# Attention stacks of 128 rows with zeros written by VectorE, and the last two second feed-forwards side by side

## The chip, the core and the metric

The kernel is one program on one core of a Trainium2 chip. A core has five engines, each with a queue of its own that runs in order: TensorE (PE; its weight loads are shown as PEld), VectorE (DVE), ScalarE (ACT), GpSimd (POOL) and SyncE (SP), which here only starts DMA transfers. Engines wait for each other through semaphores. The metric is the time of one execution on the device, in microseconds (us); lower is better. The profile is one execution, recorded instruction by instruction. For TensorE it also shows the granted clock, as a share of full speed: in this kernel it is 1.0 or 0.5.

## The reference

Four sequences of 512 tokens with 128 channels (`x`: 4 x 512 x 128, fp32) pass four blocks, each added to its input:

```python
def reference(x, ...):
    x = x + mamba_and_moe(layernorm(x))   # state-space scan, then 8 experts, top 2 of them per token
    x = x + ffn(layernorm(x))             # the first feed-forward
    x = x + attention(layernorm(x))       # 16 heads of 8 channels, causal
    x = x + ffn(layernorm(x))             # the second feed-forward, same weights
    return x

def ffn(x):                               # 128 -> 384 -> 128, weights are integers / 127
    h = silu(x @ wg.T) * (x @ wu.T)
    return h @ wd.T

def attention(x):                         # per head: scores against a latent of 64 channels
    c_kv = x @ W_dkv.T
    q_lat = einsum('bqhd,hdl->bhql', q, k_eff)
    attn = softmax(causal(einsum('bhql,bkl->bhqk', q_lat, c_kv) / sqrt(8)))
    return einsum('bhql,hld->bqhd', einsum('bhqk,bkl->bhql', attn, c_kv), v_eff)
```

## The kernel before

**Two stages.** The first stage (up to about 392 us) runs the scan: 64 steps, with the experts of finished groups of sequences ([0], then [1], then [2, 3]) and the first feed-forwards beside it. Its order on the engines is the program's. The second stage, lines 1078 to 1330, is attention; there a scheduler orders the instructions of each engine by what is ready and by priority, within what the program's order, tiles and buffers allow. Experts of the last group, the projections of the later sequences and the second feed-forwards run beside attention. They are generators in four lists (`closing`, `tokens`, `tiles`, `ends`), and each turn of a list runs its first generator up to its next `yield`.

**Attention** works in 8 units `u`, two per sequence, each with 8 heads of 512 positions. Before its units a sequence passes `project(b)`: layernorm (L153 to L167), a transposition (`transposed`, L172 to L182: into PSUM and back through ScalarE), products `pq` (L511) and `pu` (L521), and a split of the fp32 values into three bf16 parts (ScalarE L524, L525; GpSimd L526 to L528), which go out to HBM as `q_d` (L530) and `k_d` (L533).

- `fill(u)` (L1127) loads the parts back into two stacks, `qs[u % 3]` and `ks[u % 3]`: 9 parts x 8 channels = 72 rows (`NP9`). Six loads on SyncE's queue; each waits there until `q_d` or `k_d` is written, and what stands behind it waits too, expert weights among it.
- `maxima(u)`: score products `sc` over the 72 rows (L1145), a product that adds the causal mask (L1149), and the maximum of each row by VectorE (L1141). The maxima, split into three bf16 parts, are transposed, copied (`mT`, L1172), written to HBM (`m_d`, L1174) and loaded into three more rows of `qs`, 72 to 74 (L1175). The same rows of `ks` hold -1 (`below`, loaded once for each of the three stacks at the stage's start, L1103), so the product over 75 rows is the score less its maximum.
- `exps(G)`, two per unit with 4 heads each: `st` over 75 rows (L1198), the mask (L1206), the exponential by ScalarE (L1211); ten tiles each.
- `weigh(G)`: weighted sums `po` (L1225, 32 columns per head, fp32), a copy (L1235), transposition `pyt` (L1239), a copy (L1243), division (L1249, L1250), and after the last group of a sequence the sum `base` (L1255, GpSimd).

**The feed-forward** `ffn` (L428) is used twice per sequence. Per call: layernorm with an rsqrt of some ten small VectorE steps (L136 to L145, then `nm` L162) and four ScalarE steps `xn` (L167); `transposed` to `xT`; for each of three slices `pg` (L445), `pu` (L447), tanh (L449) and two VectorE steps (L321, L322); then 12 products `fpd` (L454), a copy (L459), a sum on GpSimd (L460). `last(b)` is the second feed-forward and ends with the store of the output (L468). A product in fp32 shows as two instructions in the profile.

**Order of the ends.** `begin = {3: (0,), 5: (1,), 7: (2,)}` adds `last(0)`, `last(1)` and `last(2)` to the list `ends` when units 3, 5 and 7 begin. `last(3)` runs alone at the end.

**Buffers.** The feed-forward takes its PSUM tiles from `ps_s` ("sc", two banks) and `ps` ("mm", one), its SBUF tiles from `wt`. `ps_q` ("sq") holds the score tiles of `maxima`, `ps_t` ("st") those of `exps`, two banks each.

At the stage's start VectorE also works on the end of the last sequence's scan part: `h` (L957), a norm with another rsqrt (L968, L136 to L145), the router's choice from its logits `lg` (L984, L1005 and after), and row numbers for the scatter to the experts (L252, L260).

Of the kernel before, what the change touches and what calls it, by code (L numbers as in the profile page):

```python
# [8 lines left out]
F32 = mybir.dt.float32  # L9
# [7 lines left out]
P = 128  # L17
# [20 lines left out]
def block_kernel(ctx, tc, x, rms1_w, rms2_w, in_proj_w, conv_w, conv_b, x_proj_w,  # L38
# [130 lines left out]
                scale=r[:, t : t + 1], bias=nm[:, t : t + 1],  # L169
            )  # L170

    def transposed(ps, dst, src, scale=None, beside=None):  # L172

        pt = ps.tile([P, L], F32, tag="mm" if ps is ps_m else "sc", name="pt")
        for t in range(NT):
            nc.tensor.transpose(pt[:, t * P : (t + 1) * P], src[:, t, :], ident)
            if beside:
                beside()
        if scale is None:
            nc.scalar.copy(dst, pt)  # L180
        else:
            nc.scalar.activation(dst, pt, AF.Copy, scale=scale)  # L182
# [17 lines left out]
    ]  # L200


    ps = ps_m = ctx.enter_context(tc.tile_pool(name="ps_m", bufs=1, space=PSUM))
    ps_s = ctx.enter_context(tc.tile_pool(name="ps_s", bufs=2, space=PSUM))
    wt = ctx.enter_context(tc.tile_pool(name="tiles", bufs=2))

# [218 lines left out]
        scaled(dst, src, r, less(mv[:, :, 0], r, NT))  # L425
        yield

    def ffn(src, dst):  # L428

        xn = wt.tile([P, NT, C], F32, tag="xn", name="xn", bufs=1)  # L430
        yield from layernorm(xn, src)
        xT = wt.tile([P, L], F32, tag="xT", name="xT", bufs=1)
        transposed(ps, xT, xn)
        yield
        hT = wt.tile([P, NHC, L], F32, tag="fh", name="fh", bufs=1)
        for f in range(NHC + 1):
            if f:
                halved(hT[:, f - 1, :], th, pg, pu)
            if f == NHC:
                yield  # L440
                break
            yield "sc"
            cols = slice(f * P, (f + 1) * P)
            pg = ps_s.tile([P, L], F32, tag="sc", name="pg")
            nc.tensor.matmul(pg, fwg[:, cols], xT, start=True, stop=True)  # L445
            pu = ps_s.tile([P, L], F32, tag="sc", name="pu")
            nc.tensor.matmul(pu, fwu[:, cols], xT, start=True, stop=True)  # L447
            th = wt.tile([P, L], F32, tag="th", name="th")
            nc.scalar.activation(th, pg, AF.Tanh, scale=0.5)  # L449
            yield  # L450
        pd = ps.tile([P, NT, C], F32, tag="mm", name="fpd")
        for t in range(NT):
            for f in range(NHC):
                nc.tensor.matmul(  # L454
                    pd[:, t, :], hT[:, f, t * P : (t + 1) * P], fwd[:, f, :],
                    start=(f == 0), stop=(f == NHC - 1),
                )
        o = wt.tile([P, NT, C], F32, tag="xn", name="fo", bufs=1)
        nc.scalar.copy(o, pd)  # L459
        nc.gpsimd.tensor_tensor(dst, src, o, ALU.add)  # L460
        yield
# [1 line left out]
    def first_ffn(b):  # L463
        yield from ffn(base[b], xs[b])

    def last(b):
        yield from ffn(base[b], base[b])
        nc.sync.dma_start(out[b].rearrange("(t p) c -> p t c", p=P), base[b])  # L468

    class Stream:  # L470
# [31 lines left out]
    def project(b):  # L502

        xn = wt.tile([P, NT, C], F32, tag="xn", name="axn", bufs=1)
        yield from layernorm(xn, xs[b])
        xT = wt.tile([P, L], F32, tag="xT", name="axT", bufs=1)
        transposed(ps, xT, xn)
        yield
        yield
        pq = ps.tile([P, L], F32, tag="mm", name="pq")  # L510
        nc.tensor.matmul(pq, w_qk[0], xT, start=True, stop=True)  # L511
        qk = wt.tile([P, L], F32, tag="qk", name="qk")
        nc.scalar.copy(qk, pq)
        yield
        q_d = dram0.tile([3, HS, NH, L], BF16, tag="q_d", name="q_d", bufs=2)
        k_d = dram0.tile([3, 3, HS, NH, L], BF16, tag="k_d", name="k_d", bufs=2)
        for half in range(2):
            yield
            rows = slice(half * KVL, (half + 1) * KVL)
            pq = ps.tile([P, L], F32, tag="mm", name="pu")  # L520
            nc.tensor.matmul(pq, w_up[rows, :], qk[rows, :], start=True, stop=True)  # L521
            full = wt.tile([P, L], F32, tag="full", name="full", bufs=1)
            parts = wt.tile([P, 3, L], BF16, tag="parts", name="parts", bufs=1)
            nc.scalar.copy(parts[:, 0, :], pq)  # L524
            nc.scalar.copy(full, pq)  # L525
            nc.gpsimd.tensor_tensor(full, full, parts[:, 0, :], ALU.subtract)  # L526
            nc.gpsimd.tensor_copy(parts[:, 1, :], full)
            nc.gpsimd.tensor_tensor(parts[:, 2, :], full, parts[:, 1, :], ALU.subtract)  # L528
            if half == 0:
                nc.gpsimd.dma_start(q_d.rearrange("j d h l -> (d h) j l"), parts)  # L530
            else:
                for j in range(3):
                    nc.gpsimd.dma_start(k_d[:, j].rearrange("i d h l -> (d h) i l"), parts)  # L533
            yield
        stores[b] = q_d, k_d, qk
# [63 lines left out]
    with ExitStack() as first:  # L599
# [110 lines left out]
        def front(b):  # L710
# [1 line left out]
            hn = wt.tile([P, NT, C], F32, tag="xn", name="hn", bufs=1)  # L712
            scaled(hn, xs[b], norms["r"][:, 1, b], norms["m"][:, 1, b])
            yield
            transposed(ps_s, hT[:, KW - 1 :], hn, r1w[:, 0, :], (lambda: warm(1)) if b == 0 else None)
            yield
            xi[b] = w2.tile([P, NE, L], F32, tag="xi", name=f"xi_{b}")
            sz[b] = w2.tile([P, NE, L], F32, tag="sz", name=f"sz_{b}")
# [217 lines left out]
        def close(b):  # L936
# [36 lines left out]
                )  # L973
            yield
            hsT = wt.tile([P, L], F32, tag="hsT", name="hsT", bufs=1)
            transposed(ps, hsT, hs[b], r2w[:, 0, :])
            yield
            pl = ps.tile([P, NT, NEXP], F32, tag="mm", name="pl")
            for t in range(NT):
# [46 lines left out]
        def warm(n):  # L1026

            pw = ps_x.tile([P, NE, L], F32, tag="bx", name="warm")
            for _ in range(n):
                nc.tensor.matmul(pw[:, 0, 0:P], ident, ident, start=True, stop=True)  # L1030
# [46 lines left out]
    with ExitStack() as second:  # L1077
# [15 lines left out]

        NP9 = 9 * HS
        NU = NH // 2
        UNITS = 2 * B
        qs, ks = [], []
        for i in range(3):  # L1100
            qs.append(w1.tile([96, NU, L], BF16, tag=f"qs{i}", name=f"qs{i}"))
            k = w1.tile([96, NU, L], BF16, tag=f"ks{i}", name=f"ks{i}")
            nc.sync.dma_start(  # L1103
                k[NP9 : NP9 + 3, :, :], below.unsqueeze(1).to_broadcast([3, NU, L])
            )
            ks.append(k)

        def values(b):
            va, qk = vs[b % 2], stores[b][2]
# [10 lines left out]
        def fill(u):  # L1120

            b, h0 = u // 2, (u % 2) * NU
            q_d, k_d, _ = stores[b]
            for i in range(3):
                at = slice(3 * HS * i, 3 * HS * (i + 1))
                for stack, of in ((qs[u % 3], q_d), (ks[u % 3], k_d[i])):
                    nc.sync.dma_start(  # L1127
                        stack[at], of[:, :, h0 : h0 + NU, :].rearrange("j d h l -> (j d) h l")
                    )

        def maxima(u):
# [4 lines left out]
            for t in range(NT):  # L1136
                w = (t + 1) * P
                n = L // w
                for h0 in range(0, NU, n):
                    if taken:  # L1140
                        nc.vector.tensor_reduce(*taken, AX.X, ALU.max)  # L1141
                    sc = ps_q.tile([P, L], F32, tag="sq", name="sc")
                    for h in range(h0, h0 + n):
                        c = (h - h0) * w
                        nc.tensor.matmul(  # L1145
                            sc[:, c : c + w], q[0:NP9, h, t * P : w], k[0:NP9, h, 0:w],
                            start=(h == h0), stop=False, skip_group_check=True,
                        )
                    nc.tensor.matmul(  # L1149
                        sc[:, 0 : n * w].rearrange("p (h k) -> p h k", k=w)[:, :, t * P : w],  # L1150
                        identb, maskq.unsqueeze(1).to_broadcast([P, n, P]),
                        start=False, stop=True, skip_group_check=True,
                    )
                    taken = (
                        mx[:, t, h0 : h0 + n], sc[:, 0 : n * w].rearrange("p (h k) -> p h k", k=w)
                    )
                    yield
# [14 lines left out]
            nc.scalar.copy(mT, pm)  # L1172
            m_d = dram.tile([3, NU, L], BF16, tag="m_d", name="m_d")
            nc.gpsimd.dma_start(m_d.rearrange("i h l -> (i h) l"), mT)  # L1174
            nc.gpsimd.dma_start(q[NP9 : NP9 + 3, :, :], m_d)  # L1175
            yield

        scale = float(HS) ** -0.5
# [2 lines left out]
        def exps(G):  # L1181
# [6 lines left out]
            for blocks in (  # L1188
# [7 lines left out]
                for j, kt, c in blocks:  # L1196
                    rows = slice(kt * P, (kt + 1) * P)
                    nc.tensor.matmul(  # L1198
                        pt[:, c : c + L - kt * P], k[0 : NP9 + 3, h0 + j, rows],
                        q[0 : NP9 + 3, h0 + j, kt * P : L],  # L1200
                        start=(c == 0), stop=False, skip_group_check=True,
                    )
                    got[j][kt] = p[:, c : c + L - kt * P]
# [77 lines left out]

        ends = Stream()
        streams = closing, tokens, tiles, ends
        begin = {3: (0,), 5: (1,), 7: (2,)}
        rate = {0: 0.7, 1: 0.7, 2: 0.7, 3: 0.7, 4: 0.7}
        filled, credit = 2, 0.0
        while 0 not in stores:
# [39 lines left out]
                run(more)  # L1327
        while any(stream.gens for stream in streams):
            turn(*streams)
        run(last(B - 1))  # L1330


# [54 lines left out]
```

## Time and profile before

| | us |
|---|---|
| median of 3 runs (lowest, highest) | 919.38 (919.25, 921.01) |
| the profiled execution | 916.44 |
| its span, first to last instruction | 914.7 |
| mean granted clock of TensorE | 0.872 |

The profile's page gives busy time and its share of the span per engine, and the span in 40 slices, where a digit is tenths. Two more rows of it, the busy slices of TensorE and of VectorE:

```
PE   8698697699898855976696998898768997799854
DVE  4799999899998987755364542275534266457311
```

A slice is 914.7 / 40 = 22.9 us. The scan fills slices 1 to 16, where VectorE is at 9 for long; attention is the rest. Other views are: groups of instructions (line, engine, operation, tile written and tiles read, partitions x elements, type, count, then busy time, mean ns of one, and idle time before with what ended it); the timeline of one engine (start, length, what, and in brackets the idle time before it and its releaser); stretches (length, busy time and count per engine in the order PE, PEld, DVE, ACT, POOL, then clock, DMA share, GB/s); and the chain of waits that ended last.

### The profile page before, as it was taken

What the parts mean: (1) busy time and instruction counts of PE and PEld (TensorE: products, weight loads), DVE (VectorE), ACT (ScalarE), POOL (GpSimd) and SP (SyncE); (2) the same over time, 40 slices, a digit from 0 to 9 for tenths busy, and PEclk for the clock granted to TensorE, in tenths of its full rate; (3) what the DMA queues carried; (4) which work ended last, traced back from release to release, by engine and by line L of the source; (5) the groups of instructions that cost most, each with busy time, mean ns of one, the idle gap of its engine ahead of it and who ended that gap; (6) DMA issues with size and microseconds to landing.
All of it is one profiled execution on the core that took longest, in us unless ns stands there. A gap on an engine that the chain in (4) does not pass through costs nothing. (4 is left out here: it accounts for less than half of the span.)

```text
span 914.7 us, 12164 instructions
## 1 busy us (share of the span) xinstructions
PE 736.9 (81%) x3867; PEld 436.0 (48%) x3867; DVE 584.6 (64%) x1160; ACT 409.4 (45%) x793; POOL 308.1 (34%) x242
## 2 busy tenths in 40 slices
PE   8698697699898855976696998898768997799854
PEld 4432242363466512564465576367524454365422
DVE  4799999899998987755364542275534266457311
ACT  3847556556743421342112553413436524546641
POOL 1165755765664467315103013000341402301010
PEclk9898999799999867998668999979968887989977
DMA  5167221361466314426735157627310420600000
GB/s 132 43 220 259 68 58 58 100 204 54 145 183 198 93 57 125 142 80 200 184 130 178 61 173 214 152 68 221 98 29 3 120 64 20 158 2 14 3 13 11
DMA packets 84481, 99.18 MB, mean 108 GB/s; under 512 B 10369, under 2 KB 56457, under 8 KB 83241
## 3 DMA queue, kind: packets, MB, share of 16 engines
q1 hardware_dynamic: 78881, 87.09, 32.4%
q0 software_dynamic: 4352, 10.89, 3.8%
q8 instruction: 31, 0.51, 0.2%
q10 hardware_dynamic: 1184, 0.43, 0.2%
q14 instruction: 33, 0.27, 0.1%
HBM read 76.67 MB, written 21.63 MB: 107 GB/s over the span
## 5 line engine op out<-in xcount | busy, mean ns | idle before, releaser
L922 POOL TENSOR_TENSOR hc<-hst,cs 128x1024 f32<-128x1024 f32 x64 | 150.7, 2355 | 132.1 <-issue 31.6
L867 PE MATMUL yp<-hc,ident 128*128 128x512 f32 x256 | 148.0, 708 | 48.6 <-POOL hc L922 47.4
L910 DVE TENSOR_TENSOR_SCAN hst<-da,bx 128x1024 f32<-128x1024 f32 x64 | 146.4, 2287 | 11.7 <-POOL hc L922 4.6
L1141 DVE TENSOR_REDUCE mx<-sc 128x1 f32<-128x384 f32 (+3 forms) x168 | 102.9, 636 | 59.5 <-PE sc L1149 57.4
L867 PEld LDWEIGHTS yp<-hc,ident 128*128 128x128 f32 x256 | 51.5, 216 | 129.4 <-POOL hc L922 89.3
L1211 ACT ACTIVATE p<-st 128x512 f32<-128x512 f32 x160 | 90.2, 598 | 30.0 <-PE st L1206 26.8
L847 ACT ACTIVATE da<-delta,A 128x512 f32<-128x512 f32 (+1 forms) x128 | 84.8, 714 | 34.3 <-DVE hst L910 26.6
L1145 PE MATMUL sc<-ks,qs 72*128 72x128 bf16 (+3 forms) x256 | 73.5, 347 | 14.8 <-DMA ks<-k_d 7.9
L321 DVE SCALAR_TENSOR_TENSOR thm<-thm,mpg 128x512 f32<-128x512 f32 x53 | 36.1, 681 | 68.1 <-ACT thm L382 68.0
L889 DVE TENSOR_TENSOR bx<-du,pb 128x1024 f32<-128x1024 f32 x64 | 78.2, 1223 | 2.0 <-PE pb L857 0.4
L376 PE MATMUL mpg<-xTm,wgu 128*128 128x128 f32 x424 | 66.9, 300 | 12.2 <-DMA wgu<-in_Wg_dram 7.7
L1198 PE MATMUL st<-qs,ks 75*128 75x512 bf16 (+3 forms) x256 | 63.6, 312 | 11.7 <-ACT p L1211 5.9
L376 PEld LDWEIGHTS mpg<-xTm,wgu 128*128 128x128 f32 x424 | 59.9, 212 | 21.9 <-issue 15.8
L1174 POOL DMA_DIRECT2D m_d<-mT x8 | 4.4, 552 | 183.6 <-ACT mT L1172 183.6
L376 PE MATMUL mpu<-xTm,wgu 128*128 128x128 f32 x424 | 62.7, 294 | 3.0 <-DVE mh L322 3.0
L369 ACT ACTIVATE xTm<-mpt,r2w 128x128 f32<-128x128 f32 x53 | 19.4, 366 | 100.7 <-PE mpt L367 100.7
L388 PE MATMUL mpd<-wd,mh 128*128 128x128 f32 x424 | 60.6, 287 | 1.9 <-ACT xTm L369 0.9
L376 PEld LDWEIGHTS mpu<-xTm,wgu 128*128 128x128 f32 x424 | 57.8, 210 | 5.6 <-DVE mh L322 3.3
L388 PEld LDWEIGHTS mpd<-wd,mh 128*128 128x128 f32 x424 | 54.2, 199 | 5.8 <-ACT xTm L369 3.3
L1149 PE MATMUL sc<-maskq,identb 128*128 128x128 bf16 (+2 forms) x176 | 49.3, 280 | 0.0
L382 ACT ACTIVATE thm<-mpg 128x512 f32<-128x512 f32 x53 | 31.7, 597 | 39.3 <-PE mpg L376 31.6
L321 DVE SCALAR_TENSOR_TENSOR th<-th,pg 128x512 f32<-128x512 f32 x24 | 16.5, 687 | 49.3 <-ACT th L449 49.2
(253 smaller groups left out, 1197.9 us busy)
## 6 DMA issues: line engine op xcount, KB each, us to landing
cs<-c_d SPq DMA_DIRECT2D x64, 256.0 KB
wgu<-in_Wg_dram SPq DMA_DIRECT2D x53, 256.0 KB
wgu<-in_Wu_dram SPq DMA_DIRECT2D x53, 256.0 KB
wd<-in_Wd_dram SPq DMA_DIRECT2D x53, 256.0 KB
xg<-zero SPq DMA_DIRECT2D x8, 1024.0 KB
qs<-q_d SPq DMA_DIRECT2D x24, 192.0 KB
k_d<-parts POOLq DMA_DIRECT2D x12, 384.0 KB
ks<-k_d SPq DMA_DIRECT2D x24, 192.0 KB
```

The costliest lines, as they stand in the source:

```text
L321: nc.vector.scalar_tensor_tensor(th, th, 1.0, g, ALU.add, ALU.mult)
L376: nc.tensor.matmul(pp[:, f, :], w[:, k, f * P : (f + 1) * P], rows_in, start=True, stop=True,)
L388: nc.tensor.matmul(pd, hT[:, f, :], w[:, f, :], start=(f == 0), stop=(f == NFC - 1))
L847: nc.scalar.activation(da[:, e, e:], delta[b][:, e, e:], AF.Exp, scale=A[:, e, n : n + 1])
L867: nc.tensor.matmul(yps[b][:, e, :], ident, hc[:, e, :], start=(n == 0), stop=(n == NS - 1))
L889: nc.vector.tensor_tensor(bxs[s], du[s // NS], taps[s][1].unsqueeze(1).to_broadcast([P, NE, L]), ALU.mult)
L910: nc.vector.tensor_tensor_scan(hst.rearrange("p e l -> p (e l)"), dec.pop(s).rearrange("p e l -> p (e l)"), bxs.pop(s).rearrange("p e l -> ...
L922: done = nc.gpsimd.tensor_tensor(hc, hst, cs.unsqueeze(1).to_broadcast([P, NE, L]), ALU.mult).ins
L1141: nc.vector.tensor_reduce(*taken, AX.X, ALU.max)
L1145: nc.tensor.matmul(sc[:, c : c + w], q[0:NP9, h, t * P : w], k[0:NP9, h, 0:w], start=(h == h0), stop=False, skip_group_check=True,)
L1198: nc.tensor.matmul(pt[:, c : c + L - kt * P], k[0 : NP9 + 3, h0 + j, rows], q[0 : NP9 + 3, h0 + j, kt * P : L], start=(c == 0), stop=False ...
L1211: ready[G] = nc.scalar.activation(p, pt, AF.Exp, scale=scale).ins
```

## The change

Two things are changed.

1. The stacks get 128 rows instead of 96, and both products run over them: `sc` over rows 0 to 124, `st` over all 128. The rows of the maxima and of `below` move from 72 to 74 up to 125 to 127. Rows 72 to 124 must be zero: `fill(u)`, for u below 3, writes zeros to rows 64 to 127 of both stacks with VectorE and then loads `below`, before the parts.
2. `last(2)` no longer starts with unit 7. It starts after everything else, in step with `last(3)`, which gets PSUM banks (`ps_q`, `ps_t`) and SBUF tiles (`w1`) of its own. For this `ffn` takes its pools as arguments, `transposed` takes its tag, and `th` gets an explicit two buffers.

```diff
--- before.py
+++ after.py
@@ -169,9 +169,9 @@
                 scale=r[:, t : t + 1], bias=nm[:, t : t + 1],
             )
 
-    def transposed(ps, dst, src, scale=None, beside=None):
-
-        pt = ps.tile([P, L], F32, tag="mm" if ps is ps_m else "sc", name="pt")
+    def transposed(ps, tag, dst, src, scale=None, beside=None):
+
+        pt = ps.tile([P, L], F32, tag=tag, name="pt")
         for t in range(NT):
             nc.tensor.transpose(pt[:, t * P : (t + 1) * P], src[:, t, :], ident)
             if beside:
@@ -200,7 +200,7 @@
     ]
 
 
-    ps = ps_m = ctx.enter_context(tc.tile_pool(name="ps_m", bufs=1, space=PSUM))
+    ps = ctx.enter_context(tc.tile_pool(name="ps_m", bufs=1, space=PSUM))
     ps_s = ctx.enter_context(tc.tile_pool(name="ps_s", bufs=2, space=PSUM))
     wt = ctx.enter_context(tc.tile_pool(name="tiles", bufs=2))
 
@@ -425,12 +425,12 @@
         scaled(dst, src, r, less(mv[:, :, 0], r, NT))
         yield
 
-    def ffn(src, dst):
+    def ffn(src, dst, wt=wt, two=(ps_s, "sc"), one=(ps, "mm")):
 
         xn = wt.tile([P, NT, C], F32, tag="xn", name="xn", bufs=1)
         yield from layernorm(xn, src)
         xT = wt.tile([P, L], F32, tag="xT", name="xT", bufs=1)
-        transposed(ps, xT, xn)
+        transposed(*one, xT, xn)
         yield
         hT = wt.tile([P, NHC, L], F32, tag="fh", name="fh", bufs=1)
         for f in range(NHC + 1):
@@ -441,14 +441,14 @@
                 break
             yield "sc"
             cols = slice(f * P, (f + 1) * P)
-            pg = ps_s.tile([P, L], F32, tag="sc", name="pg")
+            pg = two[0].tile([P, L], F32, tag=two[1], name="pg")
             nc.tensor.matmul(pg, fwg[:, cols], xT, start=True, stop=True)
-            pu = ps_s.tile([P, L], F32, tag="sc", name="pu")
+            pu = two[0].tile([P, L], F32, tag=two[1], name="pu")
             nc.tensor.matmul(pu, fwu[:, cols], xT, start=True, stop=True)
-            th = wt.tile([P, L], F32, tag="th", name="th")
+            th = wt.tile([P, L], F32, tag="th", name="th", bufs=2)
             nc.scalar.activation(th, pg, AF.Tanh, scale=0.5)
             yield
-        pd = ps.tile([P, NT, C], F32, tag="mm", name="fpd")
+        pd = one[0].tile([P, NT, C], F32, tag=one[1], name="fpd")
         for t in range(NT):
             for f in range(NHC):
                 nc.tensor.matmul(
@@ -463,8 +463,8 @@
     def first_ffn(b):
         yield from ffn(base[b], xs[b])
 
-    def last(b):
-        yield from ffn(base[b], base[b])
+    def last(b, *where):
+        yield from ffn(base[b], base[b], *where)
         nc.sync.dma_start(out[b].rearrange("(t p) c -> p t c", p=P), base[b])
 
     class Stream:
@@ -504,7 +504,7 @@
         xn = wt.tile([P, NT, C], F32, tag="xn", name="axn", bufs=1)
         yield from layernorm(xn, xs[b])
         xT = wt.tile([P, L], F32, tag="xT", name="axT", bufs=1)
-        transposed(ps, xT, xn)
+        transposed(ps, "mm", xT, xn)
         yield
         yield
         pq = ps.tile([P, L], F32, tag="mm", name="pq")
@@ -712,7 +712,7 @@
             hn = wt.tile([P, NT, C], F32, tag="xn", name="hn", bufs=1)
             scaled(hn, xs[b], norms["r"][:, 1, b], norms["m"][:, 1, b])
             yield
-            transposed(ps_s, hT[:, KW - 1 :], hn, r1w[:, 0, :], (lambda: warm(1)) if b == 0 else None)
+            transposed(ps_s, "sc", hT[:, KW - 1 :], hn, r1w[:, 0, :], (lambda: warm(1)) if b == 0 else None)
             yield
             xi[b] = w2.tile([P, NE, L], F32, tag="xi", name=f"xi_{b}")
             sz[b] = w2.tile([P, NE, L], F32, tag="sz", name=f"sz_{b}")
@@ -973,7 +973,7 @@
                 )
             yield
             hsT = wt.tile([P, L], F32, tag="hsT", name="hsT", bufs=1)
-            transposed(ps, hsT, hs[b], r2w[:, 0, :])
+            transposed(ps, "mm", hsT, hs[b], r2w[:, 0, :])
             yield
             pl = ps.tile([P, NT, NEXP], F32, tag="mm", name="pl")
             for t in range(NT):
@@ -1093,17 +1093,13 @@
 
 
 
-        NP9 = 9 * HS
+        NP9, MXR = 9 * HS, P - 3
         NU = NH // 2
         UNITS = 2 * B
         qs, ks = [], []
         for i in range(3):
-            qs.append(w1.tile([96, NU, L], BF16, tag=f"qs{i}", name=f"qs{i}"))
-            k = w1.tile([96, NU, L], BF16, tag=f"ks{i}", name=f"ks{i}")
-            nc.sync.dma_start(
-                k[NP9 : NP9 + 3, :, :], below.unsqueeze(1).to_broadcast([3, NU, L])
-            )
-            ks.append(k)
+            qs.append(w1.tile([P, NU, L], BF16, tag=f"qs{i}", name=f"qs{i}"))
+            ks.append(w1.tile([P, NU, L], BF16, tag=f"ks{i}", name=f"ks{i}"))
 
         def values(b):
             va, qk = vs[b % 2], stores[b][2]
@@ -1121,6 +1117,10 @@
 
             b, h0 = u // 2, (u % 2) * NU
             q_d, k_d, _ = stores[b]
+            if u < 3:
+                for stack in (qs[u], ks[u]):
+                    nc.vector.memset(stack[KVL:P], 0.0)
+                nc.sync.dma_start(ks[u][MXR:P], below.unsqueeze(1).to_broadcast([3, NU, L]))
             for i in range(3):
                 at = slice(3 * HS * i, 3 * HS * (i + 1))
                 for stack, of in ((qs[u % 3], q_d), (ks[u % 3], k_d[i])):
@@ -1143,7 +1143,7 @@
                     for h in range(h0, h0 + n):
                         c = (h - h0) * w
                         nc.tensor.matmul(
-                            sc[:, c : c + w], q[0:NP9, h, t * P : w], k[0:NP9, h, 0:w],
+                            sc[:, c : c + w], q[0:MXR, h, t * P : w], k[0:MXR, h, 0:w],
                             start=(h == h0), stop=False, skip_group_check=True,
                         )
                     nc.tensor.matmul(
@@ -1172,7 +1172,7 @@
             nc.scalar.copy(mT, pm)
             m_d = dram.tile([3, NU, L], BF16, tag="m_d", name="m_d")
             nc.gpsimd.dma_start(m_d.rearrange("i h l -> (i h) l"), mT)
-            nc.gpsimd.dma_start(q[NP9 : NP9 + 3, :, :], m_d)
+            nc.gpsimd.dma_start(q[MXR:P, :, :], m_d)
             yield
 
         scale = float(HS) ** -0.5
@@ -1196,8 +1196,8 @@
                 for j, kt, c in blocks:
                     rows = slice(kt * P, (kt + 1) * P)
                     nc.tensor.matmul(
-                        pt[:, c : c + L - kt * P], k[0 : NP9 + 3, h0 + j, rows],
-                        q[0 : NP9 + 3, h0 + j, kt * P : L],
+                        pt[:, c : c + L - kt * P], k[:, h0 + j, rows],
+                        q[:, h0 + j, kt * P : L],
                         start=(c == 0), stop=False, skip_group_check=True,
                     )
                     got[j][kt] = p[:, c : c + L - kt * P]
@@ -1281,7 +1281,7 @@
 
         ends = Stream()
         streams = closing, tokens, tiles, ends
-        begin = {3: (0,), 5: (1,), 7: (2,)}
+        begin = {3: (0,), 5: (1,)}
         rate = {0: 0.7, 1: 0.7, 2: 0.7, 3: 0.7, 4: 0.7}
         filled, credit = 2, 0.0
         while 0 not in stores:
@@ -1327,7 +1327,7 @@
                 run(more)
         while any(stream.gens for stream in streams):
             turn(*streams)
-        run(last(B - 1))
+        run(last(B - 1, w1, (ps_q, "sq"), (ps_t, "st")), last(B - 2))
 
 
 # ---- launch: one core; inputs and outputs as the reference has them ----
```

## Prediction

> **What bounds the kernel now.** I read the page first, to see whether one engine is the bound. The row of TensorE and the row of its granted clock:
>
> ```profile
> PE 736.9 (81%) x3867; PEld 436.0 (48%) x3867; DVE 584.6 (64%) x1160; ACT 409.4 (45%) x793; POOL 308.1 (34%) x242
> ...
> PEclk9898999799999867998668999979968887989977
> ```
>
> TensorE is busy for 81% of the span, but some of that is matmuls at half speed: the clock row dips to 6 and 7 from slice 15 on, which is attention (the span is 914.7 us, so a slice is 22.9 us). The sum below is made against this execution, 916.44 us: 914.7 us of span and 1.74 us around it. The median of the three runs shown is 919.38, 2.94 above it.
>
> Next I read stretches by window: the columns are length, busy time of each engine with its instruction count, granted clock, DMA share and rate. The clock turns out to change only on a grid of about 3.41 us, so I cut on that grid.
>
> ```profile
> 420.00:430.00 10.00, 4.21 (x26) 3.12 (x26) 8.28 (x21) 1.23 (x3) 8.87 (x9) 0.90 0.74 231
> 440.00:450.00 10.00, 2.30 (x21) 2.11 (x19) 1.38 (x2) 1.23 (x3) 0.00 (x0) 0.75 0.67 193
> 450.00:465.00 15.00, 13.57 (x52) 6.37 (x52) 12.06 (x20) 0.00 (x0) 0.00 (x0) 0.50 0.71 188
> 465.00:480.00 15.00, 14.75 (x95) 12.90 (x94) 8.56 (x16) 3.69 (x9) 0.00 (x0) 0.75 0.31 101
> ...
> 602.11:605.52 3.41, 3.29 (x16) 2.09 (x15) 3.09 (x8) 0.37 (x1) 0.00 (x0) 0.50 0.00 0
> ...
> 878.61:882.02 3.41, 2.74 (x28) 0.92 (x20) 0.00 (x0) 0.59 (x1) 0.00 (x0) 0.50 0.00 0
> 882.02:885.43 3.41, 0.66 (x4) 0.42 (x4) 0.66 (x3) 0.59 (x1) 1.26 (x1) 1.00 0.02 5
> ```
>
> Two things are to be seen. Between 420 and 450 every engine has idle time: one chain (layernorm of project(0), pq L511, pu L521, its split on GpSimd, k_d, the stacks) sets the time there. And TensorE, busy 3.29 of 3.41 us with matmuls of 72 rows (602.11), is still at half speed in the next windows until 608.9, while 2.74 of 3.41 us of po matmuls on 128 rows (878.61) are followed by a full clock.
>
> **Part one, the clock.** Taking all windows of the trace in order, I compared a window's matmul time with the clock of the window after. Weighted by active rows over 128, a cold window is followed by a warm one from about 0.74 of its length up, and a warm one by a cold one below about 0.37; that puts 5 of 266 windows wrong, against 12 with plain time. So 75 rows weigh about 0.59, and stacks of 128 rows, zeros included, should keep the clock up: warm-up products with the identity, nearly all zeros, raised it at 4.8 us. More rows cost nothing per matmul: of equal width, st on 75 rows takes 274 ns (L1198, 256 columns) and the mask on 128 rows 279 ns (L1206).
>
> What a higher clock gives, by stretch. 465 to 472: expert matmuls at half speed, in a window where PE is busy 14.75 of 15 us; 3 us. 450 to 465: VectorE's maxima are the limit there (12.06 of 15), 0. 585 to 588 and 605.5 to 609: PE is full there at half speed, 1.7 us each at most; I take 2.5 for both, since plain-time shares of 0.69 to 0.78 ahead of them lie at the threshold. 701 to 715: PE busy 13.26 of 14.00 at a clock of 0.51; its first window would have 0.80 and wake the next ones, leaving 10 us of which half could go; 8.1 us of ScalarE's work is in the chain beside it, so 4. The last po (rows below): 4.49 against 2.36 us, 2.1. Sum 3 + 2.5 + 4 + 2.1 = **−11.6 us**. Bounds: 0 if rows do not count, −17 with 3.3, 3.4, 5 and 2.6 for these four, 1.7 at 800 to 803 and 1 at 749 to 766.
>
> The Trainium skill ("TensorE: Matmul & The Clock Gate", Part 1, "What's actually happening") says that the gate follows how busy the PE has recently been over a window of about 3.4 us, and names no rows. The window agrees with the grid of this trace; the 602.11 row does not agree with busy time alone. By the page part one would bring nothing, and the sum of all parts would be +15.7.
>
> **Part one, the zeros.** The scheduler's order for VectorE puts the six memsets (64 rows, 2048 words of 4 bytes each) at about 393 us and after, right behind L957, between the steps of two rsqrt chains: that of the router's norm of sequence 3 (L968 to L145) and that of project(0)'s layernorm. VectorE's timeline there:
>
> ```profile
> 392.82 0.69 DVE L957 TENSOR_TENSOR h<-po,h 128x512 f32<-128x512 f32 x1 [3.00 <-PE po L951]
> 394.31 0.69 DVE L321 SCALAR_TENSOR_TENSOR th<-th,pg 128x512 f32<-128x512 f32 x1 [0.80 <-ACT th L449]
> ...
> 397.89 0.16 DVE L145 SCALAR_TENSOR_TENSOR rs_r<-rs_t,rs_r 128x4 f32<-128x4 f32 x1
> 400.69 0.87 DVE L153 BATCH_NORM_STATS2 st<-x 128x6 f32<-128x128 f32 x4 [2.63 <-POOL x L460]
> ...
> 405.31 0.16 DVE L162 SCALAR_TENSOR_TENSOR nm<-mv,rs_r 128x4 f32<-128x4 f32 x1
> ...
> 408.35 0.19 DVE L1005 TENSOR_REDUCE best<-lg 128x4 f32<-128x32 f32 x1 [1.49 <-ACT lg L984]
> ```
>
> No memset runs on VectorE in this trace. Nearest rows: L889, 128x1024 in 1223 ns, gives 2.45 us for 2048 elements; L812, 128x512 in 438 ns, gives 1.75, and the step from L695's 335 ns (384 elements) to it 1.67. I take 2.1, bounds 1.67 and 2.45. The Trainium skill ("VectorE: DVE Perf Modes", "Zero memsets can be issued as uint32 (trn2)") states one cycle per element whatever the type, so the words halve the count of bf16; no run here shows it yet.
>
> Followed by hand: memsets qs0, ks0, qs1 and ks1 stand ahead of or among the rms steps. 4 × 2.1 = 8.4, less 0.8 of idle time, plus 1.2 for project(0)'s statistics that now fall among them: rms's r is ready at 406.9 instead of 398.05. In the new order L1005, which needs the router's logits, stands ahead of project(0)'s last rsqrt steps. The logits come about 5 us after r (hs 1.4, pt 0.6, hsT 0.7, pl and lg 0.6, and the hand-overs between them), so L1005 is at 412. Behind it, ks2 (2.1), three 128x512 steps (2.1) and some twenty small ones (2.5) come before nm: 418.8 instead of 405.31. Before, pq came 6.95 us after nm, through expert matmuls; bare steps (axn 1.65, pt 0.65, axT 0.59 and hand-overs) make it 4.8, so pq starts at 423.6 instead of 412.42: +11.2. From there pu, the splits, k_d, the stacks and maxima(0) at 450.23 follow as a chain in which nothing waits for anything else, and SyncE's loads of expert weights stand behind the stacks' loads (L1127, which wait for q_d and k_d), so all behind it shifts too: **+11.2 us**; +8.6 at 1.67, +13.3 at 2.45, and 0 if later work had room. The three loads of `below` move from 386 us to behind each memset on SyncE, ahead of expert weights; those weights are for later tiles, 0, up to 1 if not.
>
> **Part two, the feed-forward of sequence 2 at the end.** The rows that matter:
>
> ```profile
> 841.78 2.36 PE L1225 MATMUL po<-p,va 128*32 128x512 f32 x32
> ...
> 876.86 4.49 PE L1225 MATMUL po<-p,va 128*32 128x512 f32 x32 [0.69 <-ACT p L1211]
> ...
> 885.32 0.87 DVE L153 BATCH_NORM_STATS2 st<-base 128x6 f32<-128x128 f32 x4 [1.38 <-POOL base L1255]
> ...
> 892.01 2.07 PE L445 MATMUL pg<-xT,fwg 128*128 128x512 f32 x2 [0.68 <-ACT xT L180]
> ...
> 901.42 2.50 PE L454 MATMUL fpd<-fwd,fh 128*128 128x128 f32 x20 [1.12 <-DVE fh L322]
> ```
>
> Today its matmuls run between 843 and 871, about 9 us of PE, partly in the 5 us that the maxima of unit 7 need for their way through HBM (to 857.4). Taken out, the 20 exps from 857.4 run at ScalarE's 0.61 each: 12.2, with po(14) 2.4 on PE and two copies (1.2) between, some 15.8: 873.1 instead of 876.8, −3.7; −5 if ScalarE's and VectorE's share before 850 is felt; I take **−4.3**. At the end, counted from base ready (885.32): statistics of two sequences, +1.2 − 0.1; xT of sequence 3 stands behind the second xn on ScalarE, +1.0; first pg 2.1 late. PE then has 12 matmul pairs at 0.88 (the chain of waits shows pg 0.88 and pu 0.91 warm) = 10.6, and 48 fpd at 2.31/20 = 5.5, where a lone one ended 11.9 us after its first pg. So 16.1 plus 2.5 for the first windows at half clock, 18.6 + 2.1 − 11.9 = +8.8, within 7.9 and 9.7. The sum on GpSimd and the out DMA of sequence 3 go beside the fpd of sequence 2, whose own take the place of the old ones. Net of the move 8.8 − 4.3 = **+4.5** (bounds 0, if the stretch at 843 to 871 gives back more than I see, and +6, from 9.7 − 3.7; the warm po is counted above). Own banks only take away waits that one ffn does not have.
>
> **Sum.** +11.2 − 11.6 + 4.5 = +4.1: 920.5 for an execution like the profiled one, 923.5 by the median.
>
> **Rivals.**
> - *Rows do not count for the clock* (or zeros do not): no gain, +15.7, **935**. For it: the 5 wrong windows. Against it: the 602.11 and 878.61 rows. Chance 0.21.
> - *The zeros are absorbed*: the delay at 393 to 424 is made up before 450, or in later idle time such as 496 to 506. Then −11.6 + 4.5 = −7.1, **912.3**, faster. It decides once the first maxima start less than about 5 us late (5.3 − 11.6 + 4.5 = −1.8). Against it: no engine has work at 442 to 450, all wait for k_d. Chance 0.18.
> - *The clock in full*: −17 instead of −11.6, **918.1**, no difference to be seen or barely faster. For it: the plain shares of 0.69 to 0.80 are near the threshold. Chance 0.16.
> - The forecast: 0.45, its own range 918.5 to 929.
>
> **How the numbers follow.** What a measurement here tells from no change is about 0.2%, 1.84 us: 917.5 to 921.2. Faster: 0.18 (absorbed) + 0.08 of the full clock + 0.04 of the forecast = 0.30. Same: 0.06 + 0.05 = 0.11. Slower: 0.36 + 0.21 + 0.02 = 0.59. The range goes from 911, the absorbed case, to 937, the case without a clock gain and a dear memset.
>
> **What would show it.** VectorE's timeline: six memsets of 1.7 to 2.45 us, nm of project(0) about 13 us later, the first sc (L1145) near 461. Clock: windows of maxima and exps at 1.0 where they were 0.5, the last po at 2.3 us. End: base of sequence 3 some 6 us earlier relative to the first sc of unit 7, and 27 us from it to the last fpd instead of 18.6. I am wrong if the half-speed windows stay with 128 rows, if the first sc starts before 455, or if the tail takes less than 24 us.

## The result and the profile after

The change makes no difference that can be measured: a median of 918.31 us (913.63 to 922.92, 20 runs) against 918.93 (913.19 to 923.24, 20 runs), ratio 0.9998, 95% interval 0.9978 to 1.0019. The forecast was slower, 923.5. Here and below medians are of all runs, while a ratio to the kernel before, with its 95% interval, leaves out runs over 1.5% above the fastest of their kernel.

The page of the changed kernel, the same two rows as before:

```profile
PE 710.8 (78%) x3859; PEld 427.2 (47%) x3867; DVE 586.8 (64%) x1166; ACT 409.2 (45%) x793; POOL 307.5 (34%) x242
...
PEclk9898899799999977888889899999979997989978
```

TensorE does the same matmuls in 710.8 us instead of 736.9, at a mean clock of 0.908 instead of 0.872 (0.908 is the highest of its 20 runs; their mean is 0.894). So something was gained, yet the span is 915.5 us against 914.7. VectorE's timeline shows where it went (the six fills are the MEMSET rows; two are left out):

```profile
394.35 0.69 DVE L957 TENSOR_TENSOR h<-po,h 128x512 f32<-128x512 f32 x1 [3.00 <-PE po L951]
395.53 1.76 DVE L1122 MEMSET qs<- 64x2048 uint32 x1 [0.48 <-issue]
...
398.58 1.76 DVE L1122 MEMSET ks<- 64x2048 uint32 x1 [0.48 <-DVE rms_v L968]
400.37 0.69 DVE L322 SCALAR_TENSOR_TENSOR fh<-th,pu 128x512 f32<-128x512 f32 x1
...
404.07 1.76 DVE L1122 MEMSET ks<- 64x2048 uint32 x1 [0.48 <-issue]
...
407.79 0.29 DVE L153 BATCH_NORM_STATS2 st<-x 128x6 f32<-128x128 f32 x1 [1.76 <-POOL x L460]
...
416.96 0.19 DVE L1005 TENSOR_REDUCE best<-lg 128x4 f32<-128x32 f32 x1 [2.38 <-ACT lg L984]
...
418.57 1.76 DVE L1122 MEMSET ks<- 64x2048 uint32 x1 [0.48 <-issue]
...
422.84 0.15 DVE L162 SCALAR_TENSOR_TENSOR nm<-mv,rs_r 128x4 f32<-128x4 f32 x1
```

What is to be seen, counted from L957, which itself starts 1.5 us later in this profile: `nm` of project(0) ends after 28.6 us instead of 12.6, pq (L511) starts after 35.2 us instead of 19.6, and the first sc after 72.6 instead of 57.4: +15.2 us. Then this delay is made up. The store of the maxima to HBM (L1174) starts at 760.72 us against 760.05 in unit 4 and at 852.54 against 850.23 in unit 7, and `base` of sequence 3 (L1255) starts at 877.62 against 884.03. The tail then takes longer. TensorE's timeline and VectorE's row at the end:

```profile
872.58 2.36 PE L1225 MATMUL po<-p,va 128*32 128x512 f32 x32 [0.69 <-ACT p L1211]
...
887.36 2.08 PE L445 MATMUL pg<-xT,fwg 128*128 128x512 f32 x2
...
899.20 5.52 PE L454 MATMUL fpd<-fwd,fh 128*128 128x128 f32 x48
```

```profile
878.91 0.87 DVE L153 BATCH_NORM_STATS2 st<-base 128x6 f32<-128x128 f32 x4 [1.37 <-POOL base L1255]
```

The last po takes 2.36 us instead of 4.49. From the statistics of the last `base` to the end of the last fpd it is now 25.8 us instead of 18.6.

A run starts attention some microseconds earlier or later even where the code before it is the same (L957 stood at 388.8 to 396.1 us in the profiles of this study). Below, "from L957" is the profiled span from the start of that instruction to the end, in which this is left out: 521.9 us before, 521.2 after. Such a figure rests on one profile of each kernel; end_only below shows that two profiles of the same instructions in the same order can be 6 us apart after 160 us.

### The profile page after: what moved, and what is told of

Its sections match the earlier page's. It is cut to its first block, busy times and chain, and to the rows that moved or that the text cites. A ratio compares the mean times of both kernels' runs of the same rounds, so it can differ in the third digit from the quotient of the medians.

```text
span 915.5 us, 12169 instructions
## 1 busy us (share of the span) xinstructions
PE 710.8 (78%) x3859; PEld 427.2 (47%) x3867; DVE 586.8 (64%) x1166; ACT 409.2 (45%) x793; POOL 307.5 (34%) x242
## 5 line engine op out<-in xcount | busy, mean ns | idle before, releaser
L847 ACT ACTIVATE da<-delta,A 128x512 f32<-128x512 f32 (+1 forms) x128 | 84.8, 714 | 35.2 <-DVE hst L910 33.4
L1145 PE MATMUL sc<-ks,qs 125*128 125x128 bf16 (+3 forms) x256 | 65.4, 312 | 19.0 <-DVE mx L1141 8.7
L1198 PE MATMUL st<-qs,ks 128*128 128x128 bf16 (+3 forms) x248 | 58.4, 299 | 14.5 <-ACT p L1211 7.6
L376 PE MATMUL mpu<-xTm,wgu 128*128 128x128 f32 x424 | 60.0, 284 | 4.6 <-DVE mh L322 4.5
L1174 POOL DMA_DIRECT2D m_d<-mT x8 | 4.4, 553 | 165.9 <-ACT mT L1172 165.9
L376 PEld LDWEIGHTS mpu<-xTm,wgu 128*128 128x128 f32 x424 | 54.8, 201 | 7.6 <-DVE mh L322 5.2
L1149 PE MATMUL sc<-maskq,identb 128*128 128x128 bf16 (+2 forms) x176 | 44.8, 255 | 0.0
L260 POOL DMA_INDIRECT xg<-hs,rows x32 | 32.4, 1012 | 36.9 <-ACT xTm L369 29.5
```

The source lines that it names most:

```text
L376: nc.tensor.matmul(pp[:, f, :], w[:, k, f * P : (f + 1) * P], rows_in, start=True, stop=True,)
L847: nc.scalar.activation(da[:, e, e:], delta[b][:, e, e:], AF.Exp, scale=A[:, e, n : n + 1])
L1145: nc.tensor.matmul(sc[:, c : c + w], q[0:MXR, h, t * P : w], k[0:MXR, h, 0:w], start=(h == h0), stop=False, skip_group_check=True,)
L1149: nc.tensor.matmul(sc[:, 0 : n * w].rearrange("p (h k) -> p h k", k=w)[:, :, t * P : w], identb, maskq.unsqueeze(1).to_broadcast([P, n, P] ...
L1198: nc.tensor.matmul(pt[:, c : c + L - kt * P], k[:, h0 + j, rows], q[:, h0 + j, kt * P : L], start=(c == 0), stop=False, skip_group_check=True,
```

## The experiments

In the first four, the rows, the zeros and the end are taken apart. They ran on one chip, where the kernel before had a median of 918.85 us, and the second four on another, where it had 916.90; across the two groups the ratios to the kernel before are what can be compared.

**zeros_alone**: the change's fills, but the old row numbers and the old end. Its instructions and their order on each engine are those of the next kernel.

```diff
-        NP9, MXR = 9 * HS, P - 3
+        NP9, MXR = 9 * HS, 9 * HS
...
-                        pt[:, c : c + L - kt * P], k[:, h0 + j, rows],
-                        q[:, h0 + j, kt * P : L],
+                        pt[:, c : c + L - kt * P], k[0:MXR+3, h0 + j, rows],
+                        q[0:MXR+3, h0 + j, kt * P : L],
...
-        begin = {3: (0,), 5: (1,)}
+        begin = {3: (0,), 5: (1,), 7: (2,)}
...
-        run(last(B - 1, w1, (ps_q, "sq"), (ps_t, "st")), last(B - 2))
+        run(last(B - 1))
```

> Undoes the rows alone: the old end (last(2) at unit 7), the six zero fills where the change has them, but products over 72 and 75 rows as before. Same instructions in the same order as rows_only on every engine. Theory A (the fills cost all of the 15 us by which the first sc is late, and the clock gives them back): the first sc near 466 and all later milestones about 15 us late, 934 us. Theory B (much of that delay is lost in idle time that was there anyway): the first sc near 466, but the delay shrinks to under 8 us by unit 4, 922 to 927 us.

Measured: 936.23 us, ratio 1.0217 (1.0144 to 1.0290); the first sc 73.1 us after L957, so +15.7; 541.1 us from L957, +19.2. Theory A: counted from L957, the delay is still 20.6 us at unit 4's store of maxima and 17.4 at unit 7's, so no idle time takes it in.

**rows_only**: part one alone, that is the changed kernel with only the last two edits of that diff (`begin` and `run`).

> Part one alone: stacks of 128 rows with zeros by VectorE, old end. Theory A: 15 us late at the first sc, some 14 us made up by the clock before unit 7 and 2 more in the last po: 917 to 919 us, so 15 below zeros_alone. Theory B: the same time, but only 4 to 8 below zeros_alone, since most of the delay goes without a faster clock.

Measured: 915.97 us, ratio 0.9998 (0.9963 to 1.0033); 520.1 us from L957. That is 20.3 us below zeros_alone by the medians and 21.0 by the profiles. Nothing but the number of rows differs, and with it which rows hold the maxima. Groups of the two kernels (mean ns of one after the comma), then a stretch of each by windows (length; PE, PEld, DVE, ACT, POOL; clock, DMA share, GB/s), first zeros_alone:

```profile
L1145 PE MATMUL sc<-ks,qs 72*128 72x512 bf16 x64 | 30.3, 476 | 2.0 <-DVE mx L1141 1.2
```

```profile
700.00:750.00 50.00, 46.12 (x227) 22.75 (x227) 16.39 (x80) 29.06 (x59) 12.60 (x14) 0.81 0.15 45
```

then rows_only:

```profile
L1145 PE MATMUL sc<-ks,qs 125*128 125x512 bf16 x64 | 24.0, 379 | 4.5 <-DVE mx L1141 3.9
```

```profile
700.00:750.00 50.00, 44.22 (x277) 23.13 (x276) 18.30 (x83) 27.90 (x55) 11.49 (x12) 0.97 0.31 85
```

A matmul over more rows takes 379 ns on average instead of 476, since more of them run at full clock: 0.97 in this stretch instead of 0.81. The rows themselves change nothing: at full clock the median is 379 ns on 72 rows as on 125, and of the 64 matmuls 29 ran at half clock on 72 rows (median 585 ns), none on 125. Theory A again.

Where the gain arises is seen from the stores of the maxima, one for each unit. Units 0, 1 and 2 of zeros_alone:

```profile
502.34 0.58 POOL L1174 DMA_DIRECT2D m_d<-mT  x1 [46.77 <-ACT mT L1172]
...
576.02 0.54 POOL L1174 DMA_DIRECT2D m_d<-mT  x1
...
670.71 0.55 POOL L1174 DMA_DIRECT2D m_d<-mT  x1 [85.26 <-ACT mT L1172]
```

and of rows_only:

```profile
501.44 0.59 POOL L1174 DMA_DIRECT2D m_d<-mT  x1 [42.66 <-ACT mT L1172]
...
570.19 0.54 POOL L1174 DMA_DIRECT2D m_d<-mT  x1
...
657.71 0.55 POOL L1174 DMA_DIRECT2D m_d<-mT  x1 [78.22 <-ACT mT L1172]
```

From L957 to the first store rows_only gains 3.4 us, from there to the second 4.9, and to the third 7.2.

**end_only**: part two alone; `MXR = 9 * HS` as above, and the fills left out:

```diff
             if u < 3:
-                for stack in (qs[u], ks[u]):
-                    nc.vector.memset(stack[KVL:P], 0.0)
```

> Part two alone: old stacks, no zeros, last(2) in step with last(3) at the end. Base of sequence 3 some 4 us earlier (no warm po), the tail 7 longer as in the changed kernel: +3, 922 us by both theories. If the lone move gains, 916 or less, part one hid a gain of part two.

Measured: 926.11 us, ratio 1.0114 (1.0051 to 1.0177); 530.5 us from L957, +8.6. Of this only +4.9 lies behind unit 7's store of maxima (69.4 us from there to the end instead of 64.5). The rest is left of +6.0 us that arose between the stores of units 0 and 1, where every engine still has the same instructions in the same order as before: the clock from 500 to 550 was 0.80 here, and 0.93 in the profile of before. TensorE's rows at the end:

```profile
877.95 3.92 PE L1223 MATMUL po<-p,va 128*32 128x512 f32 x32 [0.69 <-ACT p L1209]
...
894.27 2.07 PE L445 MATMUL pg<-xT,fwg 128*128 128x512 f32 x2
...
897.85 1.64 PE L445 MATMUL pg<-xT,fwg 128*128 128x512 f32 x2
```

With 75 rows the last po is at the low clock again (3.92 us), and so is part of the second pg (1.64; 1.02 in the changed kernel). So the move costs about 5 us there by these two profiles, 3 to 6 if the same stretch of zeros_alone (66.3) or of late_72 below (63.0) is taken for the old end. On the stacks of 128 rows it costs 0.7: from unit 7's store to the end 62.3 us in rows_only, 63.0 in the changed kernel.

**rows_late**: part one, its fills held back until project(0) has made a copy that nothing of its layernorm comes after.

```diff
-            nc.scalar.copy(full, pq)
+            marks[b, 1 + half] = nc.scalar.copy(full, pq).ins
...
-                    nc.vector.memset(stack[KVL:P], 0.0)
+                    ins = nc.vector.memset(stack[KVL:P], 0.0).ins
+                    tc.add_manual_dep(ins, marks[0, 2 if u else 1].name, sync, reason="zeros beside the split")
```

> Part one with the zeros elsewhere: still by VectorE, but each fill waits for a copy of project(0) (L525, the first half for unit 0, the second for units 1 and 2), so that none stands ahead of project(0)'s layernorm. Old end. Theory A: the first sc is back near 450 to 453 and the clock's gain stays: 903 to 908 us. Theory B: 911 to 919, since the clock alone gives 4 to 8.

Measured: 897.78 us, ratio 0.9825 (0.9770 to 0.9879), better than either theory had it; 500.7 us from L957, the first sc 57.7 after L957. The profiled execution, 891.22 us, is the fastest of its six, 6.6 below its median, so times read from this profile flatter it. VectorE's timeline shows where fills now stand:

```profile
414.96 0.17 DVE L252 CAST rows<-crowf 128x8 int32<-128x8 f32 x1
...
416.31 1.76 DVE L1123 MEMSET qs<- 64x2048 uint32 x1 [0.48 <-ACT xTm L369]
...
427.63 1.76 DVE L1123 MEMSET qs<- 64x2048 uint32 x1 [4.03 <-ACT full L526]
429.77 1.76 DVE L1123 MEMSET ks<- 64x2048 uint32 x1 [0.38 <-issue]
```

They are behind the layernorm and behind the router's row numbers (L252), and VectorE is waiting between them anyway (4.03 us ahead of the third). The same six instructions cost nothing that can be measured there (late_72 below).

The second four vary rows_late.

**late_72**: rows_late with `MXR = 9 * HS`, as zeros_alone has it; the same order on every engine as rows_late.

> The zeros where rows_late has them, but products over 72 and 75 rows: the same instructions in the same order as rows_late on every engine. If the gain of rows_late is the clock's alone (theory A), this lies within 3 us of the kernel before, and 17 to 21 above rows_late. If the later zeros gave part of it, this is below 914.

Measured: 914.94 us, ratio 0.9990 (0.9946 to 1.0034); 523.9 us from L957, 23.2 above rows_late by these profiles, but only some 15 by the ratios, 0.9990 against 0.9825; 17 to 21 was expected. The gain of rows_late is the rows' alone.

**late_96**: the same with

```diff
-        NP9, MXR = 9 * HS, P - 3
+        NP9, MXR = 9 * HS, 96 - 3
```

> As rows_late, but with products over 93 and 96 rows (rows of the maxima at 93 to 95, zeros in between; the same order again). If the clock's gate weighs matmul time by active rows, as the fit over the windows has it, 96 rows (weight 0.75) lie between: 902 to 912 us, clock 0.885 to 0.905. If it counts groups of 32 rows, of which 75 rows and 96 rows both take three, this is as late_72. If any padding does it, as rows_late.

Measured: 909.08 us, ratio 0.9909 (0.9875 to 0.9944), 520.3 us from L957: between the other two. The time lies within what was expected, the clock doesn't: 0.867 in the profile and 0.874 on average over the 12 runs, hardly above late_72's 0.863 and 0.870, where 0.885 to 0.905 was expected. The stretch from 700 to 750, in late_72, late_96 and rows_late:

```profile
700.00:750.00 50.00, 47.28 (x241) 24.41 (x240) 19.42 (x34) 19.82 (x38) 11.47 (x12) 0.81 0.31 85
```

```profile
700.00:750.00 50.00, 46.59 (x244) 23.56 (x242) 22.44 (x40) 19.12 (x36) 11.47 (x12) 0.84 0.31 84
```

```profile
700.00:750.00 50.00, 41.56 (x265) 23.77 (x257) 27.40 (x67) 17.99 (x35) 8.33 (x10) 0.93 0.27 70
```

Clock 0.81, 0.84, 0.93. This stretch is not quite the same work in each; from unit 3's store of maxima to unit 4's, which is, it takes 74.3, 71.8 and 66.5 us. Products over 75 and 96 rows occupy the same three groups of 32 rows, yet 96 rows are faster by 5.9 us, their intervals just not meeting; and padding as such is not enough. That speaks for a count finer than 32 rows. That rows count one by one is not shown: over the windows of all ten profiles, some 2,680, weights by rows predict 95 wrongly, by groups of 16 rows 97, by groups of 32 rows 103, and plain time 169 (recorded matmul time with overlaps counted once, each rule with its best two limits).

**late_ones**: rows_late with ones instead of zeros in the filler rows of qs.

```diff
-                    ins = nc.vector.memset(stack[KVL:P], 0.0).ins
+                    ins = nc.vector.memset(
+                        stack[KVL:P].rearrange("p u l -> p (u l)").bitcast(F32), 0.0 if stack is ks[u] else ONES
+                    ).ins
```

Here ONES is the fp32 number whose two halves are bf16 ones.

> As rows_late, but the filler rows of qs hold ones instead of zeros (ks still zeros, so the products add nothing). If the gate counts rows whatever they hold, within 4 us of rows_late, clock about 0.91; if it counted values that switch, clock and time would be better than with zeros, below 893.

Measured: 901.52 us, ratio 0.9817 (0.9754 to 0.9879); clock 0.888. As rows_late within the intervals, and 13.4 us below late_72 on the same chip, so rows of zeros keep the clock up as well as rows of ones.

**late_end**: rows_late with part two, that is the changed kernel with only its fills held back.

> rows_late with part two (last(2) beside last(3) at the end). With a warm clock the move took 6 us from the stretch before base of sequence 3 and added 7 to the tail: rows_late +1, 0 to +4. If a warm clock made the move a gain, 2 or more below rows_late.

Measured: 897.75 us, ratio 0.9808 (0.9741 to 0.9875); 499.6 us from L957. Not to be told from rows_late. Both beat the kernel before by nearly 2%.

## Why the prediction was wrong

The mechanisms were the right ones, and three terms of the sum were mis-sized, two of them large and of opposite sign. That the time came out no further than 5.2 us from the forecast is luck: the two large errors nearly cancel. From L957: zeros +19.2 (zeros_alone less before), rows −21.0 (rows_only less zeros_alone), the end +1.1 (after less rows_only); sum −0.7, where the forecast had +11.2 − 11.6 + 4.5 = +4.1. Each term rests on one profile of each kernel; the ratios (1.0217, 0.9998, 0.9998) give the same picture, with the end at 0 within their intervals.

- **The zeros, forecast +11.2, measured +15.2 at the first sc.** A fill takes 1.76 us and has 0.48 us of idle time before it, 2.24 in all; the 2.1 taken was near that, so the price of one was not the mistake. The step that failed is "less 0.8 of idle time, plus 1.2 for project(0)'s statistics": it kept x, the input of project(0)'s statistics, ready at 400.66 while x's own input was late. Two fills stand ahead of L322 of the first feed-forward (400.37 instead of 395.10); TensorE's fpd wait for it, the sum L460 comes after them, and the statistics wait 1.76 us more even behind four fills. So nm came 2.5 us later than forecast. The path from nm to pq, put at 4.8 us with bare steps, took 6.6, another 1.8. The bounds were too narrow as well: +8.6 and +13.3 reckon with six fills where the sum has five, which gives about +9 and +13, and 15.2 is above both. The part of zeros_alone's +19.2 above 15.7 is not settled: end_only shows the same slow stretch between units 0 and 1 without any fill.
- **The clock, forecast −11.6 with a bound of −17, measured −21.0.** That rows count was right. The step that failed is the list of stretches, read off one execution. Between zeros_alone and rows_only, the stretch up to unit 0's store gained 3.4 us (forecast 3 for 465 to 472), that between units 3 and 4 gained 4.0 (forecast 4 for 701 to 715), and that from unit 7's store to the last `base` 3.4 (forecast 2.1 for the po). But units 0 to 1 gained 4.9 where nothing was on the list, and units 1 to 2 gained 7.2 where the list had 2.5 for 585 to 588 and 605.5 to 609; units 4 to 7 gave 2.4 back. Which windows are cold differs between profiles of the same instructions at 72 and 75 rows: 500 to 550 had a clock of 0.93 in the profile of before and 0.80 in end_only. The limits 0.74 and 0.37 depend on how matmul time is counted: with recorded time, overlaps counted once, the best two for the kernel before are 0.78 and 0.52, with 7 windows wrong against 23 for plain time with its own best two, so the weighting by rows stands and the limits don't. The changed kernel can't tell the two apart, 4 windows wrong against 5. Nor is the 602.11 window of 72 rows alone: masks and expert matmuls of 128 rows are in it, and its weighted share is 0.73 by this count; the next window is still at half speed. The Trainium skill ("TensorE: Matmul & The Clock Gate", Part 1, "What's actually happening") speaks of how busy the PE was, without rows; zeros_alone against rows_only, of one order, shows that this is not enough.
- **The end, forecast +4.5, measured +0.7 to +1.1 with 128 rows and about +4.9 without.** The forecast counted the warm po with the clock and took the rest as if the two parts did not meet. On the warm clock, unit 7's load of the maxima to the ready `base` shrank by 6.3 us against rows_only instead of by 4.3 (24.1 against 30.4), and the tail grew by 7 instead of 8.8. late_end against rows_late gives the same, 6.1 and 6.5. Why the two parts of this estimate were some 2 us off each is not shown.
- **The absorbed zeros** (0.18) did not happen: zeros_alone loses all of it. **Rows that do not count** (0.21) is refuted by rows_only against zeros_alone, and by late_96 and late_ones against late_72. **The clock in full** (0.16, 918.1) comes nearest to the time, but by another sum: its gain was larger still, and so was the zeros' cost, so that nearness is luck.
- The signs named beforehand: six fills of 1.7 to 2.45 us, yes; nm 13 us later, it was 16; first sc near 461, it was 467.0; last po at 2.3, yes; base of sequence 3 some 6 us earlier against the first sc of unit 7, it was 8.8; a tail of 27 us, it was 25.8.

## What to carry over

Where a kernel's matmuls keep TensorE busy and it still falls to half clock, more rows can raise the clock, and here they cost nothing per matmul (379 ns on 72 rows and on 125); test it with the order held fixed, as zeros_alone and rows_only do. A gain can be hidden whole by where its preparation is put: look at which chain each added instruction stands in, through every engine's queue to the data it delays, and put it behind an event of that chain. A list of cold stretches from one profile can miss as much as it holds (the clock from 500 to 550 was 0.93 in one profile and 0.80 in another of the same instructions): take it from several profiles.

## What the runs showed of the hardware

- The granted clock follows matmul time weighted by active rows better than plain matmul time (95 against 169 windows wrong in the ten profiles), and filler rows of zeros count as rows of ones do. With the same instructions in the same order, 72 and 75 rows gave 0.9990 of the time before, 93 and 96 rows 0.9909, 125 and 128 rows 0.9825; with ones as filler, in nearly the same order, 0.9817.
- At one clock a matmul of 512 columns takes the same time on 72 rows and on 125: 379 ns at full clock (zeros_alone, rows_only).
- Profiles of kernels whose engines have the same instructions in the same order up to L957 reached it at 388.8 to 396.1 us, a spread of 7 us.
- VectorE's fill of 2048 words took 1.76 us, as uint32 zeros and as fp32 ones (late_ones), 0.86 ns a word, and at least 0.38 us of idle time stood ahead of each, 0.48 ahead of most. The Trainium skill ("VectorE: DVE Perf Modes", "Zero memsets can be issued as uint32 (trn2)") has one cycle per element whatever the type; that uint32 and fp32 take the same time here agrees with it, and by its clock of 0.96 GHz (same page, "Specifications") the estimate would be 2.13 us, more than measured.
